# A convolution, a two-way state-space scan and a gated feed-forward on one core: filter weights earlier on TensorE, a fourth hs buffer, last columns copied by GpSimd, gelu at other places

## The chip, the core and the metric

The kernel runs on one core of a Trainium2 chip. The core has five engines with an instruction stream each: TensorE (PE; its weight loads are shown as PEld), VectorE (DVE), ScalarE (ACT), GpSimd (POOL) and SyncE (SP). Each stream is worked through in order. A stream waits for another by semaphores. SP issues all transfers between the core's memory and DRAM here. The metric is device microseconds of one execution, and less is better.

## What is computed

The input `x` is 8 images of 64 channels and 128 x 128 pixels. Cut to what matters, the reference is

```
# layer 0, for every image
h    = leaky(conv3x3(x, w1, 64 -> 32) + b1)
w_lp = softmax(conv1x1(h, w2, 32 -> 9) + b2)            # nine filter weights a pixel
x    = x + sum_k shifted(x, k) * (delta_k - w_lp[k])
# layer 1, for every image
x_norm = layernorm_over_channels(x)
seq = res = layernorm(x_norm as 16384 steps of 64)
for i in range(2):                                      # DEPTH
    xz = in_proj(rmsnorm(seq)); u, z = split(xz)        # 128 channels each
    for d in (forwards, backwards):
        xc = silu(causal_conv1d(u)); dt, B, C = x_proj(xc)
        dt = softplus(dt_proj(dt))
        h[t] = exp(dt[t] * A) * h[t-1] + dt[t] * B[t] * xc[t]     # 128 channels x 16 states
        y_d  = (sum over states of h[t] * C[t] + D * xc) * silu(z)
    seq = seq + out_proj(y_forwards + y_backwards)
x_mamba = conv3x3(rmsnorm(seq)) + res
x = x + depthwise3x3(conv1x1(x_norm)) * x_mamba
g1, g2 = split(depthwise3x3(conv1x1(layernorm(x), 64 -> 340)))
x = x + conv1x1(gelu(g1) * g2, 170 -> 64)
```

All of it is in float32, apart from the nine filter weights, which are split in three bf16 pieces.

## The kernel before

**Chunks.** The scan is the bulk of the work. For each image there are four passes over the sequence (two layers, two directions), and each pass is cut into 16 chunks of T = 1024 steps of the sequence: 64 chunks an image, 512 in all. The 128 channels x 16 states of a chunk are laid out as 16 units of 128 partitions (32 channels x 4 states). Two units that share a state group make a pair, so a chunk has 8 pairs.

For one unit `u` of pair `k` the work is

- `drive` (L1113): GpSimd multiplies dt*x by B for a whole pair, 128 x 2048, into a `bu` buffer (four of them).
- `decay` (L1118): ScalarE makes exp(dt*A), 128 x 1024, into one of two `w` buffers in PSUM (`w_tile`, L412).
- `scan` (L1128): VectorE runs the recurrence over `w` and `bu`, starting from the unit's column in `state`.
- `keep` (L1154): ScalarE copies the last column of the result back into `state`, where the next chunk's scan of this unit will start.
- `product` (L1157): the result times C goes into the pair's `hs` buffer (128 x 2 x 1024, three buffers).
- `collect` (L1168): TensorE sums the states of the pair into `y` in PSUM. For every fourth pair it first adds the D term (dskip, L1174).

`on_pool` (L1101) says where a product runs. For six units of a chunk (0, 2, 6, 8, 10, 14) the scan writes straight into `hs` and GpSimd multiplies in place; `keep` then stands right after the scan, because the product overwrites what it reads. For the other ten, and for a unit whose scan directly follows a gelu, the scan writes over `w`, VectorE multiplies from `w` into `hs`, and `keep` stands after the product. `gelu_times` (L949) is the set of steps that hold a gelu.

**The order.** No scheduler decides it. Every piece of work is put at a time step and a phase by `at(time, phase, fn)` (L398). The phases of a step run in the order FEED, SCAN, MID, PROD, EXP, DECAY, REST (L37), and within a phase in the order of planning; chunks are planned before the background work. Chunk i starts at step 16 i; unit u is scanned at step 16 i + u. So "place 5" below is the sixth step of a chunk, and an image takes 1024 steps. `decay` of a unit stands two steps ahead of its scan, `drive` of pair k at place 2k - 5, `product` at the scan's place on VectorE and one place later, in FEED, on GpSimd, `collect` at place 2k + 3 (one later for k = 0 and 4). Work that prepares a chunk sits two chunks ahead: its convolution (L984) and evacuation at places 7 and 8, gate at 9 and 10, silu at 11, softplus at 2 of the next chunk, each of the last two with two table loads on ScalarE.

**Background work.** Beside the scans of one image run, in this order,

- Mix of the same image (from step 992 on, a chunk of rows every 13 steps): the 3x3 convolutions after the scan, and a norm;
- Ffn of the image before (FFN_AT = 1204, every 24 steps): convolutions g = 0, 2, 1 on TensorE, gelu at `GELU` = 11 steps into its chunk, products on VectorE;
- Front of the image to come (from step 593, every 24 steps): layer 0 and the norms. For nine taps k, `weight` (L572) spreads the tap's filter weight over the channels on TensorE, into the one PSUM bank "bg"; `weighted` (L582) multiplies it with the shifted input on VectorE, in MID of the next step; `gather` (L586) sums the products on TensorE.

The first image has eight of its Front chunks alone ahead of the first scan, and the last image has Mix and Ffn at other times and no Front beside it.

The `tmp` pool (L428) gives 128 x 512 buffers to the background work and to the small pieces of a chunk, twelve of them. TensorE's results for the chunks' preparation share one PSUM bank (`mm_tile`), the `y` of collect has another, "bg" and "acc" are for the background.

Of the kernel before, what the change touches and what calls it, by code (L numbers as in the profile page):

```python
# [8 lines left out]
F32 = mybir.dt.float32  # L9
# [6 lines left out]
P = 128  # L16
# [4 lines left out]
N = ROWS * W  # L21
NCH = HALF // ROWS
# [8 lines left out]
T = 1024  # L31
# [5 lines left out]
FEED, SCAN, MID, PROD, EXP, DECAY, REST = range(7)  # L37

IMAGE = 4 * NT * U
FRONT_STEP, MIX_STEP, FFN_STEP = 24, 13, 24  # L40
FRONT_AT, MIX_AT, FFN_AT = 593, 992, 1204

SILU, SOFTPLUS, GELU = 11, 18, 11

# [11 lines left out]
def kernel(ctx: ExitStack, tc: tile.TileContext, a: dict, out: bass.AP):  # L56
# [6 lines left out]
    nc = tc.nc  # L63
# [20 lines left out]
    def image(name):  # L84

        return dram([C, PW * PW + PW], name)
# [10 lines left out]
    x_img, xm_img, xn_img = image("x"), image("xm"), image("xn")  # L97
# [94 lines left out]
    with tc.tile_pool(name="wspill", bufs=1) as fp, tc.tile_pool(name="wprep", bufs=2) as pp, \  # L192
            tc.tile_pool(name="wps", bufs=4, space=PSUM) as pps:
        with tc.manual_schedule():
# [5 lines left out]
            def twice(src, n, m, k=1):  # L200

                t = pp.tile([n, k, 2, m], F32, tag=f"twice{k * m}", name="twice")
                nc.vector.tensor_copy(t[:, :, 0, :], src.rearrange("n (m k) -> n k m", k=k))
                nc.scalar.copy(t[:, :, 1, :], src.rearrange("n (m k) -> n k m", k=k))
                return t.rearrange("n k h m -> n k (h m)")

            def turned(lhsT, rhs, m, n):
                t = pps.tile([P, N], F32, tag="wps", name="turned")
                nc.tensor.matmul(t[0:m, 0:n], lhsT, rhs, start=True, stop=True)
                return t  # L210
# [76 lines left out]
            t = turned(outn[:, P:HID], ident[0:C, 0:C], REST_HID, C)  # L287
            for h in range(2):
                nc.scalar.copy(wout_b[C * h : C * h + REST_HID, :], t[0:REST_HID, 0:C])
            for (g, c0, r0, n), fn, fdn in parts:  # L290
# [7 lines left out]
                for k in range(9):  # L298
                    i, j = divmod(k, 3)
                    t = turned(fn2[:, k, :], ident[0:n, 0:n], P, n)  # L300
# [21 lines left out]
            for l in range(DEPTH):  # L322
# [8 lines left out]
                t = turned(twice(inz, DI, C)[:, 0, :], ident, P, DI)  # L331
# [8 lines left out]
                for d in range(2):  # L340
# [3 lines left out]
                    for j in range(KC):  # L344
                        t = turned(taps[:, j, :], ident, P, DI)
                        at = j if d == 0 else KC - 1 - j
# [6 lines left out]
                    t = turned(xbc, ident[0:32, 0:32], DI, 32)  # L353
# [9 lines left out]
                    for g in range(G):  # L363
                        t = turned(sel_d[:, g, :], al, P, DS)
# [33 lines left out]
    def at(time, phase, fn, *args):  # L398
        steps.setdefault((time, phase), []).append((fn, args))

    inp = ctx.enter_context(tc.tile_pool(name="in", bufs=2))
    wk = ctx.enter_context(tc.tile_pool(name="wk", bufs=2))
# [23 lines left out]
        return wk.tile([P, T], F32, tag="stage", name=name, bufs=2)  # L426

    def tmp(name):  # L428
        return wk.tile([P, N], F32, tag="tmp", name=name, bufs=12)

    def window(img, name):

# [70 lines left out]
    class Front:  # L503
# [78 lines left out]
        def weighted(self, k):  # L582
            self.t[k] = tmp("t")
            nc.vector.tensor_tensor(as_rows(self.t[k]), tap(self.xb, k), as_rows(self.wbk.pop(k)), ALU.mult)
# [69 lines left out]
        def plan(self, a):  # L654
            n1, n2, n3 = self.n1, self.n2, self.n3
            b = a - FRONT_STEP
            self.alone = a + FRONT_STEP < -2
            at(b - 5, REST, self.load_xa)
            for i in range(3):
                at(b + 1 + i, REST, self.hidden, i)  # L660
            at(b + 6, DECAY, self.hidden_out)
            at(b + 21, REST, self.logits)
            at(b + 23, DECAY, self.less_max)
            at(b + 23, DECAY, self.exps)
            at(b + 25, MID, self.sums)
            at(b + 25, REST, self.softmax)
            for i in range(3):
                at(b + 26 + 2 * i, DECAY, self.piece, i)
                if i < 2:
                    at(b + 27 + 2 * i, REST, self.less_piece, i)  # L670
            at(b + 31, REST, self.turn)
            at(b + 32, DECAY, self.turned)
            at(a + 6, REST, self.load_xb)
            for k in range(9):

                t = a + k + (k >= 3)
                at(t + 11, REST, self.weight, k)
                at(t + 12, MID, self.weighted, k)
                at(t + 13, REST, self.gather, k)
            at(a + 23, DECAY, self.filtered)  # L680
            at(a + 23, REST, self.store_x1)
            at(a + 23, REST, self.centered, acc_tile, "x1")
            at(a + 24, DECAY, self.centered_out)
            at(a + 25, REST, lambda: n1.means(bg_tile, self.sq))
            at(a + 26, DECAY, n1.means_out)
            at(a + 27, REST, n1.spread, bg_tile)
            at(a + 29, MID, self.scaled, n1)
            at(a + 29, DECAY, self.first_norm)
            at(a + 30, REST, self.pointwise)
            at(a + 31, DECAY, self.pointwise_out)  # L690
            at(a + 31, REST, self.store_rows, dw_img[self.p], "dwt")
            at(a + 31, REST, self.centered, acc_tile, "xn")
            at(a + 32, DECAY, self.centered_out)
            at(a + 33, REST, lambda: n2.means(acc_tile, self.sq))
            at(a + 34, DECAY, n2.means_out)
            at(a + 35, REST, n2.spread, acc_tile)
            at(a + 37, MID, self.scaled, n2)
            at(a + 37, DECAY, self.second_norm)
            at(a + 37, REST, self.store_h)
            at(a + 38, REST, lambda: n3.means(bg_tile, self.sq))  # L700
            at(a + 39, DECAY, n3.means_out)
            at(a + 47, REST, n3.spread, bg_tile)
            at(a + 49, MID, self.third_norm)
            at(a + 49, REST, self.store_hn)

    def plan_front(b, a):
        for i in range(NCH if b else 0):
# [6 lines left out]
    class Mix(Front):  # L714
# [40 lines left out]
        def plan(self, a):  # L755
            n1 = self.n1
            for h in range(2):
                at(a - 6 + h, REST, self.load_conv, dw_img[self.p], "dww", h)
                at(a - 4 + h, REST, self.load_conv, xm_img, "xmw", h)
            at(a - 1, REST, self.load_h)  # L760
            for i in range(3):
                at(a + i, REST, self.conv, 0, "dww", i)
                at(a + 3 + i, REST, self.conv, 1, "xmw", i)
            at(a + 3, DECAY, self.branch_out)
            at(a + 2, REST, self.load_x1)
            at(a + 5, REST, self.add_h)
            at(a + 8, MID, self.times)
            at(a + 8, REST, self.plus)
            at(a + 10, REST, self.store_x2)
            at(a + 10, REST, self.centered, bg_tile, "x1")  # L770
            at(a + 11, DECAY, self.centered_out)
            at(a + 12, REST, lambda: n1.means(bg_tile, self.sq))
            at(a + 13, DECAY, n1.means_out)
            at(a + 16, REST, n1.spread, bg_tile)
            at(a + 18, MID, self.scaled, n1)
            at(a + 18, DECAY, self.norm)
            at(a + 18, REST, self.store_rows, xn_img, "hc")

    def plan_mix(b, a, step):
        at(a - 4, REST, load_weights, 1)  # L780
# [4 lines left out]
    class Ffn:  # L785
# [57 lines left out]
                    )  # L843

        def before_taps_out(self):
            self.pre = wk.tile([P, 2, T], F32, tag="hs", name="f1", bufs=3)
            for i, bank in enumerate(self.banks):
                lo = 3 * PW * (i % 2)
                nc.scalar.copy(self.pre[:, i // 2, lo : lo + 3 * PW], bank[:, 0 : 3 * PW])
# [107 lines left out]
    class Chunk:  # L957
# [170 lines left out]
        def scan(self, u):  # L1128
            k, i = divmod(u, 2)
            if u == 0:  # L1130
                if self.first:
                    self.state = wk.tile([P, U], F32, tag="state", name="state")
                    nc.vector.memset(self.state, 0.0)
                else:
                    self.state = self.prev.state
            if i == 0:
                self.hss[k] = wk.tile([P, 2, T], F32, tag="hs", name="hs", bufs=3)
            w, hs, bu, s0 = self.ws.pop(u), self.hss[k][:, i, :], self.bus[k][:, i, :], self.column(u)
            to = hs if self.on_pool(u) else w
            if self.d == 0:  # L1140
                nc.vector.tensor_tensor_scan(to, w, bu, s0, ALU.mult, ALU.add)  # L1141
            else:
                nc.vector.tensor_tensor_scan(to[:, ::-1], w[:, ::-1], bu[:, ::-1], s0, ALU.mult, ALU.add)  # L1143
            if self.on_pool(u):
                self.keep(u, to)
            else:
                self.ws[u] = w

        def column(self, u):
# [1 line left out]
            at = G * j + 2 * gp + i  # L1151
            return self.state[:, at : at + 1]

        def keep(self, u, h):  # L1154
            nc.scalar.copy(self.column(u), h[:, T - 1 : T] if self.d == 0 else h[:, 0:1])  # L1155

        def product(self, u):  # L1157
            k, i = divmod(u, 2)
            j, hs = self.pairs[k][0], self.hss[k][:, i, :]
            c = self.cp[j // 2][:, j % 2, :]  # L1160
            if self.on_pool(u):
                nc.gpsimd.tensor_tensor(hs, hs, c, ALU.mult)  # L1162
            else:
                w = self.ws.pop(u)
                nc.vector.tensor_tensor(hs, w, c, ALU.mult)  # L1165
                self.keep(u, w)

        def collect(self, k):  # L1168

# [155 lines left out]
    for b in range(B):  # L1325
        a, last = IMAGE * b, b == B - 1
# [36 lines left out]
```

## Time and profile before

| | us |
|---|---|
| median of 3 runs (29237.95 to 29249.33) | 29244.62 |
| the profiled execution's own time | 29248.45 |
| its span, first to last instruction | 29246.5 |
| first scan starts | 500.3 |
| last scan starts | 28797.1 |

| group | count | mean ns | busy us |
|---|---|---|---|
| scan, VectorE (L1141, L1143) | 8192 | 2343 | 19195 |
| product, VectorE (L1165) | 5232 | 1221 | 6389 |
| decay, ScalarE (L1123) | 8192 | 1118 | 9158 |
| ScalarE's table loads (L68 alone) | 1137 | 1283 | 1459 |
| last column from w, ScalarE (L1155) | 5232 | 158 | 829 |
| filter weight matmul (L580) | 1152 | 431 | 490 |

How to read the lines that follow: a group's line has its source line, engine and operation, output and inputs, shape and count; then its busy time in microseconds and the mean of one in nanoseconds; then the time for which the engine stood idle just before such an instruction and what ended most of it. A line of a wait has who waited for whom, the sum in microseconds, the number of times and the longest. "issue" means that the profile shows nothing that was waited for. Times of day such as "at 12212" are microseconds from the start of the span.

### The profile page before, as it was taken

How to read it: one execution, taken by the hardware profiler on the slowest of the kernel's cores; microseconds unless marked ns; L12 is line 12 of the kernel's file. 1: busy time of each engine (PE TensorE's matmuls, PEld its weight loads, DVE VectorE, ACT ScalarE, POOL GpSimd, SP SyncE). 2: the span in 40 equal slices, each digit the busy share in tenths (PEclk: the TensorE clock that was granted, in tenths of full speed). 3: DMA queues.
4: the chain of work that ended last, by engine and by line, in shares of the span. 5: the costliest groups of instructions: out<-in, count | busy, mean ns of one | idle time of the engine just before them, and what ended most of it. 6: DMA issues, size and time to landing. Idle time of an engine off the chain costs nothing. (4 is left out here: it accounts for less than half of the span.)

```text
span 29246.5 us, 309836 instructions
## 1 busy us (share of the span) xinstructions
PE 23187.9 (79%) x97708; PEld 7296.5 (25%) x97708; DVE 27051.2 (92%) x17438; ACT 18862.0 (64%) x29130; POOL 26725.4 (91%) x8092
## 2 busy tenths in 40 slices
PE   6666888878788788887878878787787878878678
PEld 3211222223222232222322223222222222222123
DVE  4999999999999999999999999999999999999997
ACT  3666666666666666666666666666666666666663
POOL 3999899999999999999999989999899998999993
PEclk7777888988889888998889889898898988989789
DMA  4676777767877678776787767777677776777674
GB/s 123 220 248 215 226 252 243 245 216 230 259 239 241 212 236 260 239 240 209 237 262 239 237 211 246 252 240 229 218 245 251 244 224 221 250 246 243 210 251 142
DMA packets 2592261, 6762.65 MB, mean 231 GB/s; under 512 B 431270, under 2 KB 736822, under 8 KB 2589462
## 3 DMA queue, kind: packets, MB, share of 16 engines
q1 hardware_dynamic: 2590614, 6742.83, 71.8%
q8 instruction: 773, 12.66, 0.2%
q14 instruction: 874, 7.16, 0.1%
HBM read 5509.49 MB, written 1265.19 MB: 232 GB/s over the span
## 5 line engine op out<-in xcount | busy, mean ns | idle before, releaser
L1115 POOL TENSOR_TENSOR bu<-dup,bp 128x2048 f32<-128x2048 f32 x4096 | 18584.9, 4545 | 4.1 <-DMA dtp<-dt_dram 2.9
L1123 ACT ACTIVATE w<-dtp,a_neg 128x1024 f32<-128x1024 f32 x8192 | 9158.3, 1118 | 181.6 <-DMA dtp<-dt_dram 6.1
L1162 POOL TENSOR_TENSOR hs<-hs,cp 128x1024 f32<-128x1024 f32 x2960 | 7000.3, 2365 | 1596.0 <-ACT state L1155 1498.0
L1165 DVE TENSOR_TENSOR hs<-w,cp 128x1024 f32<-128x1024 f32 x5232 | 6389.4, 1221 | 244.5 <-DMA cp<-bc_dram 74.7
L1143 DVE TENSOR_TENSOR_SCAN w<-w,state,bu 128x1024 f32<-128x1024 f32 x2651 | 6211.4, 2343 | 174.3 <-ACT w L1123 162.8
L1141 DVE TENSOR_TENSOR_SCAN w<-w,state,bu 128x1024 f32<-128x1024 f32 x2581 | 6049.1, 2344 | 202.1 <-ACT w L1123 198.7
L1181 PE MATMUL y<-hs,sel_y 128*32 128x512 f32 x32768 | 5080.1, 696 | 365.4 <-POOL hs L1162 364.2
L1155 ACT COPY state<-w 128x1 f32<-128x1 f32 x5232 | 828.6, 158 | 5277.8 <-DVE hs L1165 5211.1
L1141 DVE TENSOR_TENSOR_SCAN hs<-w,state,bu 128x1024 f32<-128x1024 f32 x1515 | 3548.8, 2342 | 168.9 <-PE y L1181 65.7
L1143 DVE TENSOR_TENSOR_SCAN hs<-w,state,bu 128x1024 f32<-128x1024 f32 x1445 | 3385.8, 2343 | 309.1 <-issue 137.4
L1174 PE MATMUL y<-xc,dskip 128*64 128x512 f32 x4096 | 1465.0, 802 | 1770.8 <-ACT yv L1198 1562.4
L990 PE MATMUL xp<-hn,wx 128*128 128x512 f32 x4096 | 2379.4, 710 | 565.4 <-ACT sq L1223 352.8
L821 PE MATMUL fp<-fw,bgw 128*128 128x512 f32 (+1 forms) x5760 | 2262.4, 635 | 20.5 <-DVE gt L882 10.9
L1032 PE MATMUL dp<-xc,wdt 128*128 128x512 f32 x2048 | 1294.6, 718 | 647.5 <-ACT r L483 365.5
L1181 PEld LDWEIGHTS y<-hs,sel_y 128*32 128x32 f32 x32768 | 703.3, 115 | 3899.4 <-issue 2607.6
L1155 ACT COPY state<-hs 128x1 f32<-128x1 f32 x2960 | 565.0, 191 | 1523.5 <-DVE hs L1143 822.6
L996 ACT ACTIVATE xc<-xp,cbias 128x512 f32<-128x512 f32 x1024 | 698.3, 682 | 1294.9 <-PE xp L990 1293.9
L68 ACT ACT_TABLE_LOAD x1137 | 1458.8, 1283 | 20.7 <-PEq L1352 0.7
L595 PE MATMUL acc<-t,ident 128*128 128x512 f32 x2160 | 1296.2, 685 | 175.7 <-DVE hc L615 175.7
L827 PE MATMUL fp<-fw,bgw 64*128 64x512 f32 (+1 forms) x5760 | 1427.7, 614 | 0.0
L990 PEld LDWEIGHTS xp<-hn,wx 128*128 128x128 f32 x4096 | 841.3, 221 | 1958.9 <-issue 960.7
L1071 POOL TENSOR_TENSOR du<-dt,xc 128x1024 f32<-128x1024 f32 x512 | 1214.9, 2373 | 34.4 <-ACT dt L1045 34.4
(211 smaller groups left out, 25010.5 us busy)
## 6 DMA issues: line engine op xcount, KB each, us to landing
bp<-bc_dram SPq DMA_DIRECT2D x4096, 256.0 KB, 4.0
dup<-du_dram SPq DMA_DIRECT2D x4096, 256.0 KB, 5.1
dtp<-dt_dram SPq DMA_DIRECT2D x4096, 256.0 KB, 5.1
cp<-bc_dram SPq DMA_DIRECT2D x4096, 256.0 KB, 4.8
hn<-hn_dram SPq DMA_DIRECT2D x1024, 256.5 KB, 4.5
dt_dram<-dt SPq DMA_DIRECT2D x512, 512.0 KB, 3.0
du_dram<-du SPq DMA_DIRECT2D x512, 512.0 KB, 2.7
yf_dram<-yv SPq DMA_DIRECT2D x512, 256.0 KB, 4.1
```

What stands on the lines that cost most here:

```text
L68: nc.scalar.preload_act_table_set("natural_log_exp_and_others")
L821: nc.tensor.matmul(o, wpair[:, i, g, m], self.win[h][:, i : i + ROWS, 0:W], start=(i == 0), stop=False)
L827: nc.tensor.matmul(o, wlast[rows, i, g, m], self.win[h][rows, i : i + ROWS, lo : W + lo], start=False, stop=(i == 2),)
L990: nc.tensor.matmul(self.xp[h], wx[:, self.l, self.d, i, :], self.hn2[:, s.start + 2 * i : s.stop + 2 * i], start=(i == 0), stop=(i == 1),)
L1115: nc.gpsimd.tensor_tensor(bu, self.dup[self.pairs[k][1]], self.over_pair("bp", k), ALU.mult)
L1123: nc.scalar.activation(w, self.dtp[gp][:, i, :], AF.Exp, scale=a_neg[:, self.l, self.d, g, j : j + 1])
L1141: nc.vector.tensor_tensor_scan(to, w, bu, s0, ALU.mult, ALU.add)
L1143: nc.vector.tensor_tensor_scan(to[:, ::-1], w[:, ::-1], bu[:, ::-1], s0, ALU.mult, ALU.add)
L1162: nc.gpsimd.tensor_tensor(hs, hs, c, ALU.mult)
L1165: nc.vector.tensor_tensor(hs, w, c, ALU.mult)
L1174: nc.tensor.matmul(self.y[C * h : C * h + C, :], dskip[:, self.l, self.d, C * gp : C * gp + C], self.xc[:, s], start=True, stop=False,)
L1181: nc.tensor.matmul(self.y[lo : lo + 32, :], sel_y, hs[:, i, s], start=False, stop=(k % 4 == 3))
```

## The change

- `weight` moves from REST to DECAY of the same step, so its matmul stands on TensorE ahead of that step's REST work (collect with dskip, add_yf, gather, spread and others).
- `hs` has four buffers instead of three, `tmp` eleven instead of twelve; the scratch memory for software-made transfers is halved.
- For a unit on GpSimd, the last column is no longer copied by ScalarE right after the scan, but by GpSimd, as a copy of 128 x 1 just ahead of its product. The other units keep ScalarE's copy.
- FFN_AT goes from 1204 to 1202, so gelu falls on places 13 and 5 of a chunk where it fell on 15 and 7, and the units that are taken off GpSimd beside a gelu are 14 and 6 where they were 0 and 8. MIX_AT goes from 992 to 990.
- `hidden_out` of a Front stands one step earlier. The last Front chunk of an image has its third norm six steps earlier. A Mix chunk has its spread, scaling and stores two steps earlier.

```diff
-FRONT_AT, MIX_AT, FFN_AT = 593, 992, 1204
+FRONT_AT, MIX_AT, FFN_AT = 593, 990, 1202
...
-        return wk.tile([P, N], F32, tag="tmp", name=name, bufs=12)
+        return wk.tile([P, N], F32, tag="tmp", name=name, bufs=11)
...
-            at(b + 6, DECAY, self.hidden_out)
+            at(b + 5, DECAY, self.hidden_out)
...
-                at(t + 11, REST, self.weight, k)
+                at(t + 11, DECAY, self.weight, k)
...
-            at(a + 47, REST, n3.spread, bg_tile)
-            at(a + 49, MID, self.third_norm)
-            at(a + 49, REST, self.store_hn)
+            end = a + (49 if self.c < NCH - 1 else 43)
+            at(end - 2, REST, n3.spread, bg_tile)
+            at(end, MID, self.third_norm)
+            at(end, REST, self.store_hn)
...
-            at(a + 16, REST, n1.spread, bg_tile)
-            at(a + 18, MID, self.scaled, n1)
-            at(a + 18, DECAY, self.norm)
-            at(a + 18, REST, self.store_rows, xn_img, "hc")
+            at(a + 14, REST, n1.spread, bg_tile)
+            at(a + 16, MID, self.scaled, n1)
+            at(a + 16, DECAY, self.norm)
+            at(a + 16, REST, self.store_rows, xn_img, "hc")
...
-                self.hss[k] = wk.tile([P, 2, T], F32, tag="hs", name="hs", bufs=3)
+                self.hss[k] = wk.tile([P, 2, T], F32, tag="hs", name="hs", bufs=4)
...
-            if self.on_pool(u):
-                self.keep(u, to)
-            else:
+            if not self.on_pool(u):
                 self.ws[u] = w
...
-        def keep(self, u, h):
-            nc.scalar.copy(self.column(u), h[:, T - 1 : T] if self.d == 0 else h[:, 0:1])
+        def last(self, h):
+            return h[:, T - 1 : T] if self.d == 0 else h[:, 0:1]
...
             if self.on_pool(u):
+                nc.gpsimd.tensor_copy(self.column(u), self.last(hs))
                 nc.gpsimd.tensor_tensor(hs, hs, c, ALU.mult)
             else:
                 w = self.ws.pop(u)
                 nc.vector.tensor_tensor(hs, w, c, ALU.mult)
-                self.keep(u, w)
+                nc.scalar.copy(self.column(u), self.last(w))
...
-    nc = _bacc.Bacc("TRN2", target_bir_lowering=False, num_devices=1, dynamic_dma_scratch_size=2048)
+    nc = _bacc.Bacc("TRN2", target_bir_lowering=False, num_devices=1, dynamic_dma_scratch_size=1024)
```

More of the change, by code (lines that the diff above doesn't have):

```diff
@@ L845, in before_taps_out @@
         def before_taps_out(self):
-            self.pre = wk.tile([P, 2, T], F32, tag="hs", name="f1", bufs=3)
+            self.pre = wk.tile([P, 2, T], F32, tag="hs", name="f1", bufs=4)
             for i, bank in enumerate(self.banks):
```

## The prediction

> **What bounds the kernel now.** I read the page's busy times and groups first, then who waited for whom on VectorE (DVE) and GpSimd (POOL), then the same in stretches of single stages. Of the page:
>
> ```profile
> PE 23187.9 (79%) x97708; PEld 7296.5 (25%) x97708; DVE 27051.2 (92%) x17438; ACT 18862.0 (64%) x29130; POOL 26725.4 (91%) x8092
> L1115 POOL TENSOR_TENSOR bu<-dup,bp 128x2048 f32<-128x2048 f32 x4096 | 18584.9, 4545 | 4.1 <-DMA dtp<-dt_dram 2.9
> L1162 POOL TENSOR_TENSOR hs<-hs,cp 128x1024 f32<-128x1024 f32 x2960 | 7000.3, 2365 | 1596.0 <-ACT state L1155 1498.0
> ...
> L1155 ACT COPY state<-hs 128x1 f32<-128x1 f32 x2960 | 565.0, 191 | 1523.5 <-DVE hs L1143 822.6
> ```
>
> Two engines are busy 91 and 92% of the span, so the question for each stage is which of them has no idle time. The reader should see that GpSimd's 2960 products (L1162) wait 1498 us for ScalarE's copy of a last column (L1155), and that this copy itself waits for the scan: most of it is time in which VectorE is late. By stage (busy time in six stretches, of which I show four: no background work; Mix; Ffn; Front):
>
> ```profile
> 1205.00:2455.00 1250.00, 765.25 (x2861) 204.51 (x2860) 1191.60 (x677) 793.17 (x1169) 1247.86 (x360) 0.75 0.74 240
> 11170.00:11756.00 586.00, 460.07 (x2022) 122.50 (x2021) 551.29 (x316) 382.01 (x579) 582.31 (x178) 0.87 0.81 257
> 12019.00:12900.00 881.00, 779.48 (x3162) 243.97 (x3160) 832.65 (x507) 596.97 (x880) 811.51 (x230) 0.93 0.74 241
> 13213.00:13804.00 591.00, 444.84 (x1877) 145.21 (x1876) 535.39 (x369) 369.47 (x598) 533.46 (x174) 0.82 0.64 209
> ```
>
> After the stretch and its length the columns are the busy time (and count) of PE, PEld, DVE, ACT, POOL, then clock, DMA share, GB/s. With nothing beside the scans, and beside Mix, GpSimd is busy all the time (1247.86 of 1250, 582.31 of 586): there GpSimd sets the pace. Beside Ffn and Front it idles 8 to 10%, and VectorE with its waits sets it. VectorE's waits, over the whole span:
>
> ```profile
> DVE t L584 <- PE wb L580: 448.7, 281, 15.3
> DVE w L1141 <- ACT w L1123: 198.7, 205, 3.2
> DVE w L1143 <- ACT w L1123: 162.8, 144, 3.1
> ...
> DVE hs L1143 <- issue: 137.4, 85, 1.9
> DVE hs L1143 <- PE y L1181: 82.9, 51, 3.6
> ```
>
> and in the Ffn stretch 12019 to 12900 of image 3:
>
> ```profile
> DVE hs L1143 <- issue: 17.3, 10, 1.9
> DVE hs L1143 <- PE y L1181: 12.2, 6, 3.6
> ```
>
> **The change, part by part.** All against this execution's own 29248.45 us (span 29246.5).
>
> *GpSimd's copies: +241.* 2960 copies of 128x1 leave ScalarE (565 us, off the path of an engine that is 64% busy) and go ahead of GpSimd's products. In the built program the copy waits for the scan and the product waits for GpSimd's own copy. The trace has no such copy. GpSimd's spans are 4545 ns for 2048 columns, 2365 for 1024 and 323 for 72 (L561), which is 0.17 us fixed plus 2.13 ns a column; its smallest instruction, a 128x1 memset at the start, is 0.11 us. A copy of one column lies between, 0.14. A product that waited for L1155 began 77 ns after its end; I add that hand-off: 0.217 us a pair. Lower bound 0.11+0.035 (the gap of VectorE after its own result)=0.145; upper 0.323+0.17 (the longest hand-off seen on GpSimd)=0.49. I take the middle row because a one-column copy is nearest to the memset and the fixed part. Where it shows: I cut the trace at every 16th scan into 512 chunks; in 190 of them GpSimd idles under 0.5 us. With 5.8 products each that is 1110 pairs, 1110 x 0.217 = +241 (161 to 544). In the other 322 chunks the copy lies in GpSimd's idle time, and the way from scan to product stays as it is: 34 + 191 + 77 = 302 ns over ScalarE before, 77 + 140 + 77 = 294 after. Behind the waiting copy stand that product and the drives (L1115); drives run up to five steps ahead, so scans do not see it there.
>
> The Trainium skill ("Perfetto Trace Analysis", GPSIMD Engine Instruction) says a GpSimd span is not to be trusted and that start-to-start spacing should be used. Spacing here is 0.28 us for the 72-column product whose span is 0.32; that rule gives a copy of 0.127 and, with a free hand-off, +141 in place of +241.
>
> *Filter weights first: -282 in the loop, -20 in the prologue.* Each `weight` matmul (L580, 0.38 us) moves ahead of the same step's collect, dskip, spread and gather on TensorE. VectorE lost 448.7 us to it, 96.0 of that before the first scan (60 to 500 us), 353 in the loop. In the timeline at 13287 TensorE holds 5.9 us for ScalarE's yv, then runs dskip (2.0), collect (1.6) and spread (1.1), and only then the matmul that VectorE has waited 3.1 us for. From the bank's release to the next need there are a product (1.22) and a scan (2.25), so a matmul that is next in line is in time. At places where two conv feeds (L990) still stand ahead, about half of 1.7 us stays; that is a fifth of the total. 0.8 x 353 = -282. Front is bound by VectorE, so it comes off the span. The eight fronts ahead of the first scan are a chain of other waits; I take a fifth of 96. What is queued behind: TensorE now stands at each weight until VectorE has read the last one, and collects come later; TensorE is idle a quarter of that stretch (444.84 of 591), and the fourth hs buffer covers later collects. Bounds: -449 to +135, the latter if VectorE then meets y waits at the Ffn stretch's rate, 12.2 in 881, over Front's 24 chunks of 58 us in seven images, 9740 us.
>
> *Fourth hs buffer and gelu's place: -137.* A scan that waits for L1181 waits for a collect to free its hs buffer. Those called "issue" follow a gelu: in the timeline at 12212 a conv_out (L996) that waits for TensorE (1.4), then two table loads and three activations (4.2), delay the w of the scan two steps on by 1.5 to 1.9. Gelu moves from places 15 and 7 of a chunk to 13 and 5, where no such evacuation stands ahead. I take two thirds of 17.3 + 12.2 = 19.6 a stretch, seven images: -137. GpSimd idles 61.8 + 7.4 us there and the copies take 16 x 5.3 x 0.217 = 18, so VectorE still sets the pace. Bounds: with the waits for ScalarE's state (4.0) and gt (3.4) too, 36.9 x 7 = -258; if gelu right behind silu (place 11) costs a wait of 1.9 at each of 56, +106. The scan handed to VectorE beside a gelu is now unit 14 or 6, not 0 or 8: 112 as before. In Mix the same wait (6.7 in 586) is worth nothing, since GpSimd is the bound.
>
> *At nothing:* ScalarE's relief (bound -60: some 0.19 a burst where VectorE waits for w); eleven tmp buffers (in 56 places a t is reused two scans after its gather, three before; bound +84, one us in each of 84 such places); Mix and Ffn two steps earlier, with their loads and stores on SP's queue past two steps of chunk loads (window loads lead by four to six steps, some 14 us, and land in about 5); spread two steps earlier, hidden_out, the last chunk's norm at 43, in stretches that GpSimd covers (VectorE waited 62 us in the loop for rb; bounds -62 and +62). The DMA scratch serves nothing: only hardware queues are listed.
>
> Sum: 241 - 282 - 20 - 137 = -198, so 29,048; the median lies 4 us under this execution: 29,045.
>
> **Rivals.**
> 1. *The copy is dear (slower).* Place: the 190 chunks that GpSimd binds. Gains of 439 break even at 439/1110 = 0.395 us a pair; at the 0.49 bound +544 - 439 = +105: 29,350. For: small GpSimd work never ran back to back with a wait on itself here. Against: 0.32 us for 72 columns leaves little for one.
> 2. *TensorE takes the wait (slower).* Weights gain nothing because TensorE stands for VectorE at each (it did so for 427.5 us already) and feeds and collects come late: 241 - 137 = +104: 29,349. Against: its idle quarter.
> 3. *Ffn gains nothing*, GpSimd taking VectorE's place: 241 - 302 = -61: 29,185, at the edge of no change.
> 4. *More comes off:* copies at 0.145 (+161), all loop waits (-353), Ffn -258: -450: 28,795.
> The change does what it says: in the built program's order the weights stand ahead of the spread, and 2960 copies are there.
>
> **How the numbers follow.** Forecast 0.48 (28,880 to 29,185), rival 1 0.16, rival 2 0.16, rival 3 0.10, rival 4 0.10. What a measurement can tell from no change is about 0.2%, 58 us. Faster: forecast, rival 4 and a third of rival 3, 0.61; same: the rest of rival 3 and edges, 0.10; slower 0.29. The range runs from rival 4 to beyond both slower ones, 28,800 to 29,420; the forecast's own is 28,880 to 29,185.
>
> **What would show it.** L580's wait on VectorE down from 448.7 to under 170; "issue" and L1181 waits of scans halved; GpSimd's copies at 0.11 to 0.17 us with 0.08 before the product; Mix and bare chunks longer by 1.3 us (53.2 to 54.5 in Mix), Front chunks shorter by 1 to 2. Wrong if bare chunks grow by over 2.4 us, or if VectorE's waits for L580 reappear under L990, L996 or hs.

## The result and the profile after

| | us | ratio to before (95% interval) |
|---|---|---|
| before, median of 4 runs | 29243.26 (29237.95 to 29249.33) | |
| after, median of 4 runs | 28836.42 (28807.60 to 28855.68) | 0.9861 (0.9849 to 0.9874) |
| span of the profiled execution before, after | 29246.5, 28833.6 | |

The change saves 1.39%, 407 us by the medians and 413 by the spans. I had forecast 198 off the span: the right sign, and inside my whole range (28,800 to 29,420), but half the size, and 44 us below the forecast's own 28,880. Of the page after, the busy times and two of GpSimd's groups:

```profile
PE 22961.3 (80%) x97708; PEld 7243.9 (25%) x97708; DVE 27012.9 (94%) x17438; ACT 18542.2 (64%) x26170; POOL 27201.8 (94%) x11052
L1162 POOL TENSOR_TENSOR hs<-hs,cp 128x1024 f32<-128x1024 f32 x2960 | 6963.1, 2352 | 243.3 <-DMA cp<-bc_dram 5.1 <-PE y L1181 1.2 <-PE op L1210 0.4
L1161 POOL COPY state<-hs 128x1 f32<-128x1 f32 x2960 | 552.2, 187 | 367.0 <-DVE hs L1142 178.4 <-DVE hs L1144 150.2 <-PE acc L595 37.6
```

GpSimd's product no longer waits 1596 us, since its own copy (L1161) now does the waiting, 367 us. The 243.3 us ahead of the product are 2960 hand-offs from the copy. GpSimd's and VectorE's shares are now both 94%. The same four stretches after the change (no background work, Mix, Ffn, Front; columns as before):

```profile
1190.00:2440.00 1250.00, 761.22 (x2750) 196.95 (x2751) 1158.54 (x658) 756.14 (x992) 1238.80 (x491) 0.74 0.71 233
11030.00:11620.00 590.00, 448.51 (x1940) 117.98 (x1936) 537.01 (x306) 365.85 (x499) 584.88 (x238) 0.85 0.77 249
11840.00:12720.00 880.00, 773.79 (x3216) 242.24 (x3214) 851.61 (x519) 596.30 (x809) 849.20 (x324) 0.96 0.73 245
12960.00:13545.00 585.00, 453.08 (x1949) 148.16 (x1947) 566.63 (x388) 384.55 (x568) 579.88 (x250) 0.84 0.68 221
```

In the first two VectorE got through less in the same time (1158.54 of 1250, before 1191.60): GpSimd sets the pace there and now has the copies to do as well. Its own busy time fell there (1238.80 of 1250, before 1247.86) because the hand-offs count as idle: 140 copies with 0.08 us behind each make 11 us. In Front VectorE's work went from 535 of 591 to 567 of 585, and GpSimd's to 580: beside the first half of Front both engines are now nearly full. VectorE's waits over the whole span:

```profile
DVE t L584 <- PE wb L580: 253.2, 141, 11.8
DVE hc L615 <- PE rb L490: 171.7, 54, 11.3
DVE w L1142 <- ACT w L1124: 144.4, 105, 5.8
...
DVE w L1144 <- ACT w L1124: 85.6, 69, 2.8
```

The wait for the filter weight went from 448.7 to 253.2. The scans' waits for "issue" and for collect (L1181) are no longer among the large ones. The waits for a decay (w) went from 198.7 and 162.8 to 144.4 and 85.6, which my working had not asked for; with the scans that write into hs, and wait for a decay too, they went from 379 to 316. TensorE, which had stood 427.5 us ahead of filter weight matmuls until VectorE had read the weight before, now stands nearly twice as long there:

```profile
PE wb L580 <- DVE t L584: 810.3, 484, 3.2
```

Where the time went shows when the trace is cut at the first scan of each chunk and the stages of all images are added up (chunks are numbered within an image; microseconds):

| stage | chunks | before | after | difference |
|---|---|---|---|---|
| ahead of the first scan | | 500.3 | 481.8 | -18.5 |
| Front, image 0 (chunks 0 to 11) | 12 | 705.1 | 654.0 | -51.2 |
| no background, image 0 (12 to 36) | 25 | 1298.8 | 1332.6 | +33.7 |
| Front, first half (37 to 47) | 77 | 4506.5 | 4218.0 | -288.5 |
| Front, second half (48 to 60) | 91 | 5292.6 | 5259.5 | -33.1 |
| 61 to 63 | 21 | 1143.8 | 1118.8 | -25.0 |
| Mix (0 to 10, and 11) | 84 | 4460.4 | 4618.0 | +157.6 |
| Ffn (12 to 34) | 161 | 8755.0 | 8521.6 | -233.4 |
| between Ffn and Front (35, 36) | 13 | 660.8 | 677.0 | +16.2 |
| image 7 from chunk 36, and the last chunk | 28 | 1923.2 | 1952.4 | +29.2 |

The stages bound by GpSimd lost about what I had said. Ffn and Front, with chunks 61 to 63, gained 631 us together, where I had said 419. Front's two halves differ by a factor of nearly nine, and nothing in my working told them apart: chunks 32 to 47 are the first pass of a layer, 48 to 63 the second.

### The profile page after: what moved, and what is told of

Its sections match the earlier page's. It is cut to its first block, busy times and chain, and to the rows that moved or that the text cites. A ratio compares the mean times of both kernels' runs of the same rounds, so it can differ in the third digit from the quotient of the medians.

```text
span 28833.6 us, 311734 instructions
## 1 busy us (share of the span) xinstructions
PE 22961.3 (80%) x97708; PEld 7243.9 (25%) x97708; DVE 27012.9 (94%) x17438; ACT 18542.2 (64%) x26170; POOL 27201.8 (94%) x11052
## 5 line engine op out<-in xcount | busy, mean ns | idle before, releaser
L1116 POOL TENSOR_TENSOR bu<-dup,bp 128x2048 f32<-128x2048 f32 x4096 | 18545.3, 4534 | 9.9 <-DMA dup<-du_dram 2.4
L1162 POOL TENSOR_TENSOR hs<-hs,cp 128x1024 f32<-128x1024 f32 x2960 | 6963.1, 2352 | 243.3 <-DMA cp<-bc_dram 5.1
L1144 DVE TENSOR_TENSOR_SCAN w<-w,state,bu 128x1024 f32<-128x1024 f32 x2651 | 6212.3, 2343 | 113.9 <-ACT w L1124 85.6
L1142 DVE TENSOR_TENSOR_SCAN w<-w,state,bu 128x1024 f32<-128x1024 f32 x2581 | 6049.4, 2344 | 173.0 <-ACT w L1124 144.4
L1181 PE MATMUL y<-hs,sel_y 128*32 128x512 f32 x32768 | 4983.5, 688 | 694.4 <-POOL hs L1162 693.6
L991 PE MATMUL xp<-hn,wx 128*128 128x512 f32 x4096 | 2332.5, 698 | 757.3 <-ACT xc L997 320.9
L822 PE MATMUL fp<-fw,bgw 128*128 128x512 f32 (+1 forms) x5760 | 2196.5, 625 | 242.7 <-DMA fw<-xn_dram 230.9
L1181 PEld LDWEIGHTS y<-hs,sel_y 128*32 128x32 f32 x32768 | 714.7, 115 | 4242.9 <-issue 2328.2
L991 PEld LDWEIGHTS xp<-hn,wx 128*128 128x128 f32 x4096 | 795.2, 212 | 2161.9 <-issue 861.6
L580 PE MATMUL wb<-wt,sel_k 65*128 65x512 bf16 x1152 | 509.3, 448 | 919.5 <-DVE t L584 810.3
```

The source lines that it names most:

```text
L822: nc.tensor.matmul(o, wpair[:, i, g, m], self.win[h][:, i : i + ROWS, 0:W], start=(i == 0), stop=False)
L991: nc.tensor.matmul(self.xp[h], wx[:, self.l, self.d, i, :], self.hn2[:, s.start + 2 * i : s.stop + 2 * i], start=(i == 0), stop=(i == 1),)
L1116: nc.gpsimd.tensor_tensor(bu, self.dup[self.pairs[k][1]], self.over_pair("bp", k), ALU.mult)
L1181: nc.tensor.matmul(self.y[lo : lo + 32, :], sel_y, hs[:, i, s], start=False, stop=(k % 4 == 3))
```

## The experiments

Eleven kernels ran. The quoted expectations weigh theories against each other. S says that ScalarE, relieved of the copies, delivers its decays earlier; T, that TensorE's order alone made Front's gain; J, that the parts need each other, and later that the fourth `hs` buffer pays in Front once the weights go first; H, that `hidden_out`'s earlier place made the part that was not forecast. The others (K, P, R, W) are told where they come up. The medians of before were 29243 to 29283 us in the different batches, so runs of different batches are compared by their ratios. 0.1% is 29 us, and an interval is about 41 us to either side.

| kernel | median, us | ratio (95% interval) |
|---|---|---|
| before + weights first | 29091.14 | 0.9938 (0.9923 to 0.9953) |
| before + GpSimd's copies | 29515.30 | 1.0086 (1.0069 to 1.0103) |
| before + fourth hs buffer | 29303.99 | 1.0008 (0.9998 to 1.0017) |
| before + all moved times | 28941.03 | 0.9886 (0.9871 to 0.9901) |
| before + hidden_out's time alone | 29012.91 | 0.9916 (0.9901 to 0.9931) |
| before + moved times but hidden_out's | 29149.53 | 0.9964 (0.9951 to 0.9976) |
| before + weights first + all moved times | 28724.13 | 0.9819 (0.9804 to 0.9833) |
| after, last columns copied by ScalarE | 28607.01 | 0.9778 (0.9763 to 0.9792) |
| after, hidden_out back | 29066.70 | 0.9929 (0.9912 to 0.9945) |
| after, weights last | 29063.36 | 0.9924 (0.9909 to 0.9939) |
| after, ScalarE's copies, weights first in first passes only | 28541.90 | 0.9747 (0.9732 to 0.9761) |

### One part at a time

**Weights first, alone.**

```diff
-                at(t + 11, REST, self.weight, k)
+                at(t + 11, DECAY, self.weight, k)
```

> The kernel before with nothing changed but the filter weights in DECAY. Theory S (the Front gain beyond the forecast comes from ScalarE, which no longer stops for a scan before each next decay): this alone gives what was forecast for the weights, some -280 in the loop and -20 ahead of it, so 28,945, and VectorE's waits for ScalarE's w in Front stay at 1.8 a chunk. Rival T (TensorE's order alone): the whole Front gain, -400, 28,850, and the waits for w go with it. Rival J (the parts need each other): with three hs buffers later collects hold the scans, the gain is under 150, over 29,095, and scans wait for L1181 in Front.

Ratio 0.9938, some 181 us. The two halves of Front went opposite ways: chunks 37 to 47 lost 225 us, image 0's front 35, and chunks 48 to 60 grew by 70. None of the three theories had that. S and T asked for some 300 and 400 us. J's time is near, but not its reason: the scans of chunks 37 to 47 wait for collect's L1181 for 0.07 us a chunk. Most of the waits for w stayed (1.80 us a chunk before, 1.25 now, in chunks 38 to 47), so it is not the order of the weights that removes them.

**GpSimd's copies, alone.**

```diff
-            if self.on_pool(u):
-                self.keep(u, to)
-            else:
+            if not self.on_pool(u):
                 self.ws[u] = w
...
+                nc.gpsimd.tensor_copy(self.column(u), hs[:, T - 1 : T] if self.d == 0 else hs[:, 0:1])
                 nc.gpsimd.tensor_tensor(hs, hs, c, ALU.mult)
```

> The kernel before with only the last columns of GpSimd's scans copied by GpSimd. All theories: bare chunks 52.0 to 53.5 and Mix 53.2 to 54.8, +240 in the stretches that GpSimd binds. Theory S: Front -115 and Ffn -95 from ScalarE's relief, 29,275 in all, waits for w in Front down from 1.8 to 0.3 a chunk. Rival T: nothing in Front and Ffn, 29,485. Rival J: in between, as VectorE then waits for the filter weights and hs instead.

Ratio 1.0086: 251 us dearer, and no stage of Front or Ffn got clearly shorter (chunks 37 to 47: +25; 48 to 60: -21; 16 to 31: +44). So theory S falls, and T's time (29,485) comes closest. GpSimd's groups in this kernel:

```profile
L1161 POOL TENSOR_TENSOR hs<-hs,cp 128x1024 f32<-128x1024 f32 x2960 | 6966.4, 2354 | 258.1 <-DMA cp<-bc_dram 20.3 <-POOL state L1160 2.0 <-DMA bp<-bc_dram 0.4
L1160 POOL COPY state<-hs 128x1 f32<-128x1 f32 x2960 | 555.6, 188 | 1003.4 <-DVE hs L1143 637.5 <-DVE hs L1141 359.5 <-PE zp L1005 2.9
```

A copy of one column has a span of 188 ns, and the product behind it starts 79 ns later at the earliest: 0.267 us a pair (here, as in the prediction's sums, a copy and its product, not two units). At the same time GpSimd's other spans are a little shorter, the product 2354 ns for 2365 and the drive 4534 for 4545. With eight drives and 5.8 such pairs a chunk that is 5.8 x 0.267 - 8 x 0.011 - 5.8 x 0.011 = 1.40 us a chunk, and in the 149 chunks of the stages bound by GpSimd (image 0 without background, Mix, 11, 35 and 36, image 7) 208 us; those stages grew by 205.

**Fourth hs buffer, alone.**

```diff
-        return wk.tile([P, N], F32, tag="tmp", name=name, bufs=12)
+        return wk.tile([P, N], F32, tag="tmp", name=name, bufs=11)
...
-                self.hss[k] = wk.tile([P, 2, T], F32, tag="hs", name="hs", bufs=3)
+                self.hss[k] = wk.tile([P, 2, T], F32, tag="hs", name="hs", bufs=4)
...
-    nc = _bacc.Bacc("TRN2", target_bir_lowering=False, num_devices=1, dynamic_dma_scratch_size=2048)
+    nc = _bacc.Bacc("TRN2", target_bir_lowering=False, num_devices=1, dynamic_dma_scratch_size=1024)
```

(The last image's `f1`, which uses the same pool, has its count raised too.)

> The kernel before with only four hs buffers, eleven tmp buffers and the smaller scratch. Theories S and T: the scans' waits for L1181 go (149 us), those of Ffn (some 95) come off, those of Mix are worth nothing as GpSimd binds there: 29,150 to 29,180. Rival J: the wait goes over to the next one (w, gt, filter weights), under 30 us off, 29,215 to 29,260.

Ratio 1.0008, no change, as J had said. VectorE's waits in an Ffn stretch of image 3 (12040 to 12920), to set beside the prediction's two lines of before:

```profile
DVE hs L1143 <- ACT w L1123: 17.5, 10, 1.9
DVE hs L1143 <- ACT state L1155: 7.6, 14, 0.8
```

The 12.2 us for collect are gone, and the ten waits of 17.3 that had been called "issue" now end with a decay: 17.5, again ten times and 1.9 at most. With the buffer free, ScalarE is seen to be what those scans wait for. The buffer alone buys nothing: the scans then wait for a decay instead.

**All moved times, alone.**

```diff
-FRONT_AT, MIX_AT, FFN_AT = 593, 992, 1204
+FRONT_AT, MIX_AT, FFN_AT = 593, 990, 1202
...
-            at(b + 6, DECAY, self.hidden_out)
+            at(b + 5, DECAY, self.hidden_out)
...
-            at(a + 49, MID, self.third_norm)
+            at(end, MID, self.third_norm)
...
-            at(a + 18, MID, self.scaled, n1)
+            at(a + 16, MID, self.scaled, n1)
```

> The kernel before with only the moved times: Ffn and Mix two steps earlier with gelu at places 13 and 5, the spread in Mix, hidden_out and the last norm. Theories S and T: the waits named issue after a gelu (146 us) go by two thirds, Ffn -80 to -100: 29,145 to 29,165. Rival J: gelu two steps after silu costs what it saves, 29,220 to 29,300, with waits for w after silu of over 1 us a chunk.

Ratio 0.9886, 333 us: the largest of the four parts, more than any theory had, and four times the 80 us that my sum had for gelu's place (two thirds of 17.3, seven times). Ffn (12 to 34) lost 145 us, but Front 222, where only `hidden_out` and the last chunk's norm had moved.

### hidden_out

Moved alone, and left out of the moved times.

```diff
-            at(b + 6, DECAY, self.hidden_out)
+            at(b + 5, DECAY, self.hidden_out)
```

> The kernel before with one line changed: hidden_out of a Front one step earlier. Theory H (two activations, L526 and L527, hold the PSUM bank acc that the pointwise matmul L624 needs, and what stands behind it on TensorE, the next chunk's bc, is late, ScalarE waits for it, and softplus and w come late): this alone gives the Front part of the moved times, -220 to -230 (-80 in chunks 37 to 47, -140 in 48 to 60), about 29,040; TensorE's wait of L624 for ScalarE's ha from 322 to under 40 us. Rival K (the Front gain comes from the last norm or from Mix and Ffn ending earlier): under 20 us here.

> The kernel before with the moved times (Ffn, Mix, spread, last norm) but hidden_out where it was. Theory H: only the Ffn part is left, -145 in Ffn and +40 to +70 in Mix and the quiet chunks, so 29,140 to 29,200, Front within 20 us of the kernel before. Rival K: as all moved times together, about 28,940.

Alone: 0.9916, 246 us, of which 234 in Front (37 to 47: -83; 48 to 60: -141; image 0: -10) and none in Ffn. Without it the other times give 0.9964, 105 us, and the two halves of Front stay where they were (+5.2 and +0.2). Theory H is shown. What it removes is in TensorE's waits, here of before and then of the kernel with hidden_out's time alone:

```profile
PE dwp L624 <- ACT ha L527: 322.4, 112, 5.4
```

```profile
PE dwp L624 <- ACT ha L527: 37.2, 31, 1.4
```

L526 and L527 are the two activations of `hidden_out`. They read `hp` out of the one PSUM bank "acc", and in the same step the pointwise matmul `dwp` (L624) of the Front chunk two before it wants that bank. Of 128 Front chunks 112 met the wait. One of them in before, on TensorE, ScalarE and VectorE (start, duration, engine, line, operation; in brackets the idle time ahead of it and what ended it):

```profile
13273.00 1.80 PE L624 MATMUL dwp<-hc,bgw 128*128 128x512 f32 x2 [3.33 <-ACT ha L527]
13274.72 1.92 PE L1051 MATMUL bcp<-xc,wbc 128*32 128x512 f32 x4
```

```profile
13272.27 0.68 ACT L527 ACTIVATE ha<-hp,b 64x512 f32<-64x512 f32 x1
13276.69 0.58 ACT L1058 COPY bc<-bcp 64x512 f32<-64x512 f32 x1 [2.65 <-PE bcp L1051]
```

```profile
13279.08 2.36 DVE L1143 TENSOR_TENSOR_SCAN w<-w,state,bu 128x1024 f32<-128x1024 f32 x1 [1.36 <-ACT w L1123]
```

The same place with hidden_out a step earlier:

```profile
13171.68 1.13 PE L624 MATMUL dwp<-hc,bgw 128*128 128x512 f32 x2
13173.78 1.05 PE L1051 MATMUL bcp<-xc,wbc 128*32 128x512 f32 x4 [0.97 <-ACT dt L1039]
```

```profile
13175.22 0.57 ACT L1058 COPY bc<-bcp 64x512 f32<-64x512 f32 x1
```

Four steps of a queue: hidden_out's second activation ends at 13272.95; TensorE, which has stood 3.33 us for it, does dwp; behind dwp stand the bcp matmuls (L1051) of a scan chunk to come, which needed nothing of it; ScalarE waits 2.65 us for bcp, and the decays behind that copy reach VectorE 1.36 us late. In the later kernel dwp starts without a wait, bcp waits 0.97 us for ScalarE's dt (L1039) and not for dwp, and the copy does not wait. The Trainium skill ("TensorE: Matmul & The Clock Gate", The mechanism) says that matmuls start and end strictly in program order; here bcp, from 13274.72, behind dwp, from 13273.00, agrees. In the ten chunks 38 to 47 of all images VectorE's wait for w fell from 1.80 us a chunk to 0.30; in chunks 48 to 60 it fell from 1.14 to 0.11, and the wait for the filter weight from 1.20 to 0.82.

The same edit undone in the changed kernel:

```diff
-            at(b + 5, DECAY, self.hidden_out)
+            at(b + 6, DECAY, self.hidden_out)
```

> The changed kernel with hidden_out back at its old unit (b + 6), all else changed. Theory H (hidden_out's place is worth the same whatever the weights do): TensorE's wait before the pointwise matmul, 16.6 us in all, is back at some 300 us and the time is 180 to 230 us longer, 29,020 to 29,070 us. Rival (weights first hides the late eviction too, so the two gains overlap): 100 us longer or less, under 28,940 us.

Ratio 0.9929 against 0.9861: 0.68%, 199 us. TensorE's wait ahead of dwp is back (16.6 us in 17 places in the changed kernel):

```profile
PE dwp L624 <- ACT ha L527: 311.3, 112, 5.5
```

So the rival (under 100 us) falls, but in part it holds. In the first half of Front hidden_out's place is worth the same with the weights first (91 us) as with the weights last (83). In the second half it is worth 63 where it was worth 141: the waits for w go in both cases, but with the weights first the wait for the filter weight rises from 1.07 to 1.56 us a chunk at the same time.

### The copies, and the fourth buffer with the rest

After, with the last columns on ScalarE again (the edit below); and before with the weights first and all moved times, thus the same without the fourth buffer (and with twelve tmp):

```diff
-            if not self.on_pool(u):
+            if self.on_pool(u):
+                nc.scalar.copy(self.column(u), self.last(to))
+            else:
                 self.ws[u] = w
...
-                nc.gpsimd.tensor_copy(self.column(u), self.last(hs))
                 nc.gpsimd.tensor_tensor(hs, hs, c, ALU.mult)
```

> The changed kernel with ScalarE copying the last columns again, right after the scan; all else as changed. Theory P (the copies cost 0.25 us a pair wherever GpSimd binds, and buy nothing): at least the 240 us of bare chunks and Mix come back, 28,600, and more where GpSimd has become the bound beside Front and Ffn (some 340 chunks in all, down to 28,350). Rival R (ScalarE's relief is needed beside Front, where it took part in the gain): Front longer by 50 to 120, 28,650 to 28,720 or more.

> The kernel before with the weights in DECAY and the moved times, nothing else: three hs buffers, twelve tmp, ScalarE's copies. Theory J (late collects hold the scans once the weights go first, so the fourth hs buffer is worth something only together with them): 60 to 140 longer than the kernel with four hs buffers and ScalarE's copies, and scans wait for L1181 beside Front. Rival (four buffers are worth nothing, as alone): the same time within 0.2%.

Ratios 0.9778 and 0.9819. Without the copies the changed kernel is 0.83%, some 243 us, faster, so they cost what they cost alone and buy nothing. The fourth buffer, worth nothing alone, is worth 0.41%, some 120 us, on top of the rest: 85 in chunks 16 to 31, where without it a scan or a VectorE product waited for collect's matmul for 0.53 and 0.51 us a chunk, and 19 in Mix. So J's time comes out (it had 60 to 140), but its reason does not: Front differs by 14 to 16 only, its scans hardly wait for collect (0.06 us a chunk), and the buffer pays in Ffn. There no filter weight runs, so its neighbour is gelu's new place.

### The weights, by pass

The changed kernel with the weights last again:

```diff
-                at(t + 11, DECAY, self.weight, k)
+                at(t + 11, REST, self.weight, k)
```

> The changed kernel with the filter weights last in TensorE's order again, all else changed. Theory W: chunks 37 to 47 go from 4218 to about 4423 us, image 0's front and prologue lose some 60, chunks 48 to 60 gain 100; time about 29,000 us. Rival (weights first is worth the full 300 us that I predicted, in both passes): time about 29,140 us.

Ratio 0.9924 against 0.9861: weights first are worth 0.63%, some 184 us. By stage, chunks 37 to 47 grew by 230, image 0's front by 40, and chunks 48 to 60 shrank by 111. Then the changed kernel with ScalarE's copies, and the weights first in the first pass alone:

```diff
-                at(t + 11, DECAY, self.weight, k)
+                at(t + 11, DECAY if (t + 11) % IMAGE < 48 * U or t + 11 < 0 else REST, self.weight, k)
```

> The changed kernel with ScalarE's copies, and the filter weights first in TensorE's order only where their step falls in chunks 0 to 47 of an image (a first pass); in chunks 48 to 63 they stand last, as before. Theory W (weights first pays in the first pass and costs in the second, where the wait on TensorE is already gone with hidden_out's new place): chunks 48 to 60 come down from 5252 us to about 5152, chunks 37 to 47 stay at 4184, time about 28,505 us. Rival (the second pass is dear for another part of the change): chunks 48 to 60 stay at 5250, time about 28,607 us.

Ratio 0.9747 against 0.9778 with the weights first everywhere, and the fastest of all kernels here: 2.5% under before. Chunks 48 to 60 went from 5251.6 to 5145.6 and chunks 37 to 47 stayed at 4184, as theory W said. One place that shows why the second pass is the worse for it is unit 9 of chunk 60 of image 3. TensorE and VectorE with the weights first everywhere:

```profile
14157.92 0.59 PE L580 MATMUL wb<-wt,sel_k 65*128 65x512 bf16 x1 [3.19 <-DVE t L584]
14158.30 1.91 PE L1192 MATMUL y<-yf,ident 128*128 128x512 f32 x2
14160.01 1.61 PE L595 MATMUL acc<-t,ident 128*128 128x512 f32 x2
14161.45 1.88 PE L991 MATMUL xp<-hn,wx 128*128 128x512 f32 x4
...
14168.93 0.38 PE L580 MATMUL wb<-wt,sel_k 65*128 65x512 bf16 x1 [0.94 <-ACT r L483]
```

```profile
14164.02 2.33 DVE L1142 TENSOR_TENSOR_SCAN w<-w,state,bu 128x1024 f32<-128x1024 f32 x1
14169.34 0.69 DVE L584 TENSOR_TENSOR t<-xb,wb 128x512 f32<-128x512 f32 x1 [2.99 <-PE wb L580]
```

and with the weights last in this pass:

```profile
14139.17 1.98 PE L991 MATMUL xp<-hn,wx 128*128 128x512 f32 x4 [0.38 <-ACT sq L1224]
...
14146.89 0.38 PE L580 MATMUL wb<-wt,sel_k 65*128 65x512 bf16 x1
```

```profile
14144.14 2.33 DVE L1142 TENSOR_TENSOR_SCAN w<-w,state,bu 128x1024 f32<-128x1024 f32 x1
14147.30 0.69 DVE L584 TENSOR_TENSOR t<-xb,wb 128x512 f32<-128x512 f32 x1 [0.83 <-PE wb L580]
```

A weight matmul that is next in line holds TensorE until VectorE has read the weight before (3.19 us), and add_yf (L1192), which only a second pass has, the gather and the next chunk's convolution (L991) come after it. So the first L991 starts 2.6 us ahead of this scan, where it starts 5.0 ahead of it in the other order. ScalarE's evacuation and its r (L483) are late with it; r reads the bank that the next weight needs; and VectorE waits 2.99 us where it waited 0.83. This place comes in chunks 48, 51, 54, 57 and 60 of every image, but the wait is not always so long: 2.99 us in 14 of the 35 and 1.39 in the others, where the other order has 0.83 in 23 and 1.74 in 12. Over chunks 48 to 60, VectorE's wait for L580 is 1.48 us a chunk in the one order and 0.86 in the other; the waits for decays go from 0.43 to 0.08 and the one for rb from 0.26 to 0.08. Together that is 1.15 us a chunk, 105 us in 91 chunks: all of the difference. Of the waits for L580 with the weights first, 64 of 135 us stand at units 1 and 6 of chunks 50, 53, 56 and 59, where the other order has none; this timeline does not explain those.

## Why the prediction was half the size

By its own terms, in us off the median; the runs' column is the removal of one part from the changed kernel, in ratios times 29,244:

| term | predicted | shown |
|---|---|---|
| GpSimd's copies | +241 | +243 |
| weights first, with the prologue | -302 | -184 |
| fourth buffer and gelu's place (Ffn) | -137 | some -233 to -266 |
| hidden_out, within "at nothing" | 0, bounds 62 to either side | -199 (alone -246) |
| sum | -198 | -407 |

The value for the fourth buffer and gelu's place is Ffn's stage difference, -233, or what the other three leave of the sum, -266; the parts do not add up exactly.

**The step that failed stands under "At nothing": "hidden_out, the last chunk's norm at 43, in stretches that GpSimd covers".** Both halves of it were wrong. Hidden_out stands in Front, and my own table of stretches showed GpSimd idle there (533 of 591). And I bounded it by VectorE's wait for rb, 62 us, which has nothing to do with it: the work that waits for hidden_out is a matmul, and TensorE's waits of before had a row of 322.4 us for it. That row stands in the same list of waits as the 427.5 us that my rival 2 quotes. I had weighed VectorE's and GpSimd's waits only, because those two set the pace, and put down TensorE's idle quarter as slack. The wait reaches VectorE by way of two more queues: the bcp matmuls behind dwp, and ScalarE's copy of bcp with the decays behind it. It alone is some 200 of the 208 us that the forecast lacked; the two other errors, 118 us too much for the weights and 96 to 129 too little for Ffn, cancel, which is luck. The other moved times that I had taken at nothing were small: in the kernel with hidden_out left where it was, Mix grew by 35 us, chunks 35 and 36 grew by 15, and chunks 61 to 63 shrank by 14.

**The copies:** right in the sum, by two errors that cancel. A pair cost 0.267 us less what the shorter spans gave back, 0.24, where I had 0.217; and the stages that GpSimd binds are 149 chunks (208 us), not 190; the rest of the 243 fell outside them. The copy's span, 187 ns, lies above the 0.11 to 0.17 that I had named; the memset was the poorer neighbour, the fixed part of 0.17 the better one. The spacing rule that I weighed from the Trainium skill ("Perfetto Trace Analysis", GPSIMD Engine Instruction) gave +141, 100 us under what the runs showed. It did not fail as a rule: from the start of a copy to the start of its product the mean is 0.269 us. I had taken a span and a spacing of a 72-column product that did not wait for GpSimd's own last result, and given that rule a free hand-off. Mix chunks went from 53.2 to 54.8 us (I had said 54.5).

**Weights first:** right in kind, mis-sized for one pass. I had 0.8 of the loop's wait gone, everywhere. In the first pass it held: chunks 38 to 47 went from 2.92 us of wait for L580 a chunk to 0.30, a tenth. In the second it rose from 1.20 to 1.56: rival 2 (TensorE takes the wait, and feeds come late) is what happened there, and its price, shown by the pass-wise order, is 106 us. "Its idle quarter" was no argument against it, since that idle time is not where add_yf and the convolution stand. I had said that the wait for L580 would fall under 170; it is 253.2. The prologue's -18.5 agrees with my -20. Over all kernels, the six with the weights first there begin their first scan at 480 to 501 us (489 in the mean) and the seven others at 499 to 514 (506). So the size is borne out in the mean, but one pair of kernels does not show it.

**Fourth buffer and gelu's place:** the mechanism was right, the size too small by about 100, because the stretch that I took seven times is not all of Ffn. From 12019 to 12900 are chunks 16 to 31 of image 3, and those changed by 133 us over all images, where I had 137. The other 100 us came off chunks 12 to 15 and 32 to 34, which hold five of an image's sixteen gelus; VectorE's waits there went from 91 us to 11. (Some 20 us of it came back in chunk 11, into which Ffn's start has moved further.) Even in chunks 16 to 31 my two thirds came out by luck: the 1.08 us a chunk of "issue" and 0.67 of collect are both wholly gone, but some 0.6 more is waited for w. Nor do the two parts split as I had put it. Gelu's place brings the gain (Ffn -145 with the moved times alone), the buffer nothing by itself and some 85 once gelu has moved.

**ScalarE's relief** (bound -60) is nothing, as taken; rival 3 (Ffn gains nothing) fell, and rival 1 too, since 0.24 us a pair lies well under the 0.395 at which it broke even. Rival 4 gave the time best (28,795), by the wrong reason: its copies at +161 and Ffn at -258, with no hidden_out.

## What to carry to other kernels

A step that only evacuates a PSUM bank is not free because its engine and its stretch look slack: look up who waits for that bank on TensorE, and what stands behind the waiting matmul in its queue, even if TensorE is far from being the bound. "Earlier in an in-order queue" helps the one at the front and charges all that stand behind it, so price it by stage: the same order was worth 230 us in one pass and cost 106 in the next. And test the parts of a change one by one, from before and from after: here one part cost 243 us and hid in a change that was faster as a whole, and another paid only with its neighbour.

## What was not expected of the hardware

GpSimd needs 187 to 188 ns for a copy of a single column and at least 79 ns more before its own next instruction that waits for it may start: 0.27 us for one column, beside 2.35 us for a product of 1024. GpSimd's other spans moved with the place of the copies: a drive took 4534 ns with them on GpSimd and 4545 (before) or 4557 (after, with ScalarE's copies) without; why was not tried.
